# Attention over a graph's edges: tables in rows of 30 and 60, edges in two loads, a shorter last round with a branch behind it

## The chip, the cores and the metric

The kernel runs on one core of a Trainium2 chip. Its time is the device time of one execution in microseconds (us). TensorE (PE) multiplies matrices, VectorE (DVE) and ScalarE (ACT) work element by element, GpSimd (POOL) here mostly issues gathers, and SyncE (SP) issues the plain transfers. The core has 16 DMA engines; a transfer is split over some of them.

## The reference

One layer of graph attention over N = 12500 nodes with 256 features and E = 200000 edges, which come sorted by their target dst.

```python
h = jnp.maximum(_layernorm(x, axis=-1), 0.0)
q = (h @ Wq + bq).reshape(n, HEADS, D)          # HEADS 8, D 32
k = (h @ Wk + bk).reshape(n, HEADS, D)
v = (h @ Wv + bv).reshape(n, HEADS, D)
logits = jnp.einsum('ehd,ehd->eh', q[dst], k[src]) / jnp.sqrt(jnp.float32(D))
seg_max = jax.ops.segment_max(logits, dst, num_segments=n)
expv = jnp.exp(logits - seg_max[dst])
denom = jax.ops.segment_sum(expv, dst, num_segments=n)
attn = expv / denom[dst]
agg = jax.ops.segment_sum(attn[:, :, None] * v[src], dst, num_segments=n)
y = h + jax.nn.gelu(agg.reshape(n, HID) + (h @ Wskip + bskip), approximate=False)
return x + _layernorm(y) * gamma + beta
```

The sources src are drawn evenly over the nodes; dst is 12500 u² for u drawn evenly from 0 to 1, so the first nodes have many edges and the last ones few.

## The kernel before

**Three stages.** First, project (in gnn_kernel) makes h and, with 98 blocks of 128 nodes, the keys and values: two products of 128 x 512 a block on PE (L243), added to the bias by DVE into kvo, and stored as kv_tab and h_tab. Beside it make_plan works out from src and dst, mostly on DVE and POOL, who handles which edge when: load_edges reads the 200000 edges into 127 partitions of 1566 and a rest of 1118, DVE casts them (L418), indirect loads fetch for each step its first edges (dch from dst, sch from src), and from these come the lists of the gathers idx, the first node of each step and stream (d0_row), the rows of finished nodes (slot_row) and a flag, which SyncE and the others read at the end of the plan (values_load): it chooses between walk_streams and a general path, walk_partitions.

Second, walk_streams. The list of edges is cut into S = 8 streams of 25000, and the loop goes over c = 0 to 65 (NST = 66 steps); a step takes 383 new edges of every stream, as K = 3 tiles j of 128 (the last step has two). For each tile POOL issues eight indirect gathers, one for each stream, of 128 rows of keys and values (gather, L1010), into one of five buffers kv. Since dst is sorted, a step of one stream meets few target nodes: a window of 32 nodes in streams 0 to 3 ("narrow") and 64 in streams 4 to 7 ("wide"). windows loads their rows of h (hw), PE makes the queries from them, spread repeats these for the edges with one-hot matrices (to_e), times multiplies with the keys (DVE, L1053), total sums within heads (L1062), maxima finds the running maximum of a node's edges by two scans (L1082 is the first) and ACT takes the exponential, weigh multiplies the values by these weights into vw (L1109; L1114 is a small second product of the first tile), and add_up sums over the edges of a node with the other one-hot matrix (to_n) on PE. The sums are copied to sums_w and stored to table in DRAM: from each window all rows but the first, so 31 and 63 of them. A node cut by the boundary of two steps is carried on by copying row 0's sums into the next step.

```python
              keep(nc.sync.dma_start(table[s, ds(g["nodes"][s], w - 1), :],
                                     g["sums"][at + 1:at + w, i, :]))
```

A store writes rows of nodes beyond the step's last one as well; the next step overwrites them, so SyncE's stores to one part of table stay in order. The plan checks that no step meets more nodes than a store holds (far and bad in make_plan, against w - 1); otherwise the flag chooses the general path.

**Pairs.** A finished node still needs division by its sum, the skip product, gelu, the second normalization and the output store. These go by slots: 104 slots of 128 nodes, taken two at a time as 52 Pairs. Pair m is due in step FIN_FIRST + m * FIN_RATE // 32, that is from step 10 on in most steps one; its work is spread over three steps (fetch; turn, divisors, skip, divide, add, gelu, stats, root as "pair"; factors, normal, shifted, scale, store as "before"). The streams begin their blocks of 128 nodes anew, so the number of slots filled depends on where the streams' boundaries fall; it is counted in the plan (gvu[:, 0, F - 1:]), and slots beyond it repeat the last one. Pairs 46 to 51 come due only after the last step; the class Last handles these six, whose rows of x and h are loaded in step 64 (fetch_rows) and whose sums after the last stores (fetch_sums, L913).

**Order.** keep ties every instruction of the loop to the one before on its engine, so each engine works in the order in which the code is written. The gathers on POOL are outside keep, but POOL runs them in program order, and a gather waits until its buffer is free: the third of step c + 1, gather(c + 1, 2), stands behind weigh(c, 0). In the plan the order on each engine is instead made by a scheduler, which works from its own estimates of how long each instruction and transfer takes; some instructions of project are tied by hand (behind).

**The last round** (after the loop, c = 65): pair is m = 45 and before is m = 44. The order on every engine is: before.factors and normal; the one-hot products; before.shifted, scale, store(0); the last pairs' first turn; maxima; then exp, weigh and add_up, the stores of table; before.store(1); the fetches of sums; pair's ending; and the six last pairs, first all up to gelu, then all endings, two output stores for each (L882). The six take their PSUM banks from qe_ps (four), xt_ps and ag_ps (bank).

Of the kernel before, what the change touches and what calls it, by code (L numbers as in the profile page):

```python
# [28 lines left out]
F32 = mybir.dt.float32  # L29
# [22 lines left out]

FIN_FIRST = 10
FIN_RATE = 39
PAD = 127.0
# [8 lines left out]
def gnn_kernel(ctx: ExitStack, tc: tile.TileContext, x, src, dst, Wq, bq, Wk, bk, Wv, bv,  # L64
# [248 lines left out]
    flag = pl.tile([1, 2], I32, name="flag")  # L313
# [12 lines left out]
    fits = nc.values_load(flag[0:1, 0:1], min_val=0, max_val=1)  # L326
    with tc.If(fits > 0) as branch:
        table = dram.tile([S, NT, SUMS], F32, name="table")
        walk_streams(tc, N, HID, NST, KL, ident, idx, d0_row, slot_row, near, near_n, e_tab, pen_tab,
                     h_tab, kv_tab, table, x, out, w_q, w_s, one_row, b_q3, b_s3, b_o3,  # L330
                     gam, eps)
# [45 lines left out]
def load_edges(nc, pool, a, E, C, fill, name):  # L377
# [4 lines left out]
    nc.gpsimd.dma_start(t[:full], a[:full * C].rearrange("(p c) -> p c", c=C))  # L382
# [15 lines left out]
def make_plan(tc, pool, ep, psum, src, dst, N, LEN, NST, SLACK, NT, dram, ident, flag, idx, d0_row,  # L398
              slot_row, e_tab, pen_tab, products):

# [104 lines left out]
    for i, w in enumerate((WNN, WN)):  # L505
        nc.vector.tensor_scalar(bad[:, 0, i * 4:i * 4 + 4], bad[:, 0, i * 4:i * 4 + 4],
                                float(w - 1), None, op0=OP.is_gt)
# [108 lines left out]
    for i, w in enumerate((WNN, WN)):  # L616
        nc.vector.tensor_reduce(far[:, i:i + 1], dl[:, i * 4:i * 4 + 4, :], AX.XY, OP.max)
        nc.vector.tensor_scalar(far[:, i:i + 1], far[:, i:i + 1], float(w - 1), None,
# [51 lines left out]
    nc.vector.tensor_scalar(w2[:, 4:5], gvu[:, 0, F - 1:], float(M), None, op0=OP.is_gt)  # L670
    nc.vector.tensor_reduce(w2[:, 5:6], w2[:, 0:5], AX.X, OP.max)
# [69 lines left out]
def walk_streams(tc, N, HID, NST, KL, ident, idx, d0_row, slot_row, near, near_n, e_tab, pen_tab, h_tab,  # L741
# [174 lines left out]
    with ExitStack() as es:  # L916
# [199 lines left out]
        def add_up(c, i, tiles=range(K)):  # L1116
# [28 lines left out]
            for s in streams:  # L1145
                _, at, w = where(s)
                keep(nc.sync.dma_start(table[s, ds(g["nodes"][s], w - 1), :],
                                       g["sums"][at + 1:at + w, i, :]))
# [5 lines left out]
        rest = due.get(NST - 1, []) + due.get(NST, [])  # L1154

# [27 lines left out]
        assert len(rest) <= 6  # L1183
# [8 lines left out]
        def bank(i):  # L1192
            def get():
                if i > 3:
                    return (xt_ps.tile([P, 512], F32, name="ps_x") if i == 4 else
                            ag_ps.tile([P, 2 * HID], F32, name="ps_a")).rearrange(
                                "p (b d) -> p b d", b=2)
# [13 lines left out]
        for c in range(NST - 1):  # L1211
# [48 lines left out]
            if c == NST - 2:  # L1260
                for i in range(6):
# [51 lines left out]
        if before:  # L1313
            before.factors()
            before.normal()
# [6 lines left out]
        if before:  # L1322
            before.shifted()
        if tiles_of(c) == K:
            turn(c, K - 1)
        if before:
            before.scale()
            before.store(0)
        if pair:
            pair.divisors()  # L1330
# [414 lines left out]
```

## Time and profile before

| what | us |
|---|---|
| median of 15 runs (lowest, highest) | 2402.76 (2393.57, 2417.73) |
| the profiled execution, its own time | 2398.33 |
| its span in the profile | 2396.5 |
| busy: PE, DVE, POOL, ACT | 1866.0, 1935.0, 1593.1, 1076.7 |
| 1576 gathers on POOL (L1010) | 1548.7 |
| 197 large products of weigh on DVE (L1109) | 444.7, 2.285 each |
| 394 products of times on DVE (L1053) | 467.8, 1.219 each |

The span is the time from the first to the last instruction in the profile; the execution's own time is a little longer. A group's row in the profile gives its busy time, the mean of one instruction, and the idle time of its engine just before, with what ended most of it. A wait is put down to the last of the events that the instruction needed. The chain of waits is followed back from the end: at each step to what released the instruction, or to the one before it on its engine. POOL issues the gathers, and between two of them lies issue time that is not counted as busy. A transfer's row gives its issue; when it has landed is read from what waits for it, or from the semaphore that its engines count up.

### The profile page before, as it was taken

To read this page: it belongs to the slowest core of one execution; us is meant where nothing else is said; L and a number is where in the kernel's file an instruction comes from. 1 tells how busy PE (TensorE), PEld (TensorE's weight loads), DVE (VectorE), ACT (ScalarE), POOL (GpSimd) and SP (SyncE) were. 2 spreads that over 40 slices of the span, in tenths; PEclk is the share of its full clock that TensorE was granted. 3 is DMA by queue.
4 is the path that set the end of the run, shared out by engine and by line. 5 is a ranking of instruction groups with operands and counts; after the bars stand their busy time and mean duration, and the time that the engine had idled before them with its cause. 6 is when DMAs were issued, how large, how long until landed. Compare 5 with 4: busy or idle time off the path is not lost.

```text
span 2396.5 us, 34967 instructions
## 1 busy us (share of the span) xinstructions
PE 1866.0 (78%) x10240; PEld 1077.8 (45%) x10240; DVE 1935.0 (81%) x2228; ACT 1076.7 (45%) x2527; POOL 1593.1 (66%) x1646
## 2 busy tenths in 40 slices
PE   7999776777877787777777787877787777787776
PEld 3444443444444444444444444444444444444443
DVE  7889577777788878778788888788788888788784
ACT  3432233333455445445455454454454554454443
POOL 2210677777777777777777777777777777777730
PEclk9999778777899889889999898898988998988987
DMA  7865777778877878887888888887888888788862
GB/s 276 301 248 206 239 244 244 243 244 256 261 251 252 266 251 257 271 259 245 262 263 255 270 261 260 263 269 240 267 258 266 259 267 256 255 269 256 260 194 69
DMA packets 274030, 601.06 MB, mean 251 GB/s; under 512 B 47239, under 2 KB 164212, under 8 KB 271648
## 3 DMA queue, kind: packets, MB, share of 16 engines
q0 software_dynamic: 128736, 423.23, 55.9%
q1 hardware_dynamic: 144562, 175.02, 21.9%
q8 instruction: 84, 1.38, 0.2%
q14 instruction: 118, 0.97, 0.1%
q10 hardware_dynamic: 530, 0.47, 0.1%
HBM read 514.42 MB, written 84.11 MB: 250 GB/s over the span
## 4 chain that ended last, share of the span: by engine, by line
POOL 25%; DMA 23%; DVE 18%; PE 15%; issue 14%; ACT 4%; DVEq 0%; SPq 0%; ACTq 0%; POOLq 0%
POOL kv L1010 25%; DMA kv<-kv_tab,idx 20%; DVE vw L1109 6%; PE ps_kv L243 5%; DVE prod L1053 5%; PE ps_qe L1043 3%; DVE L L1062 2%; PE ps_a L829 2%; PE ps_hot L871 1%; DVE st L845 1%; DMA x_in<-in_x_dram 1%; ACT L950 1%; DMA e_tab<-row 1%; DMA table<-sums_w 1%; DVE sums L841 1%
## 5 line engine op out<-in xcount | busy, mean ns | idle before, releaser
L1010 POOL DMA_INDIRECT kv<-kv_tab,idx x1576 | 1548.7, 983 | 522.6 <-issue 428.1
L1043 PE MATMUL ps_qe<-qw,to_e 64*128 64x256 f32 x3152 | 484.3, 438 | 227.0 <-DVE prod L1053 227.0
L1109 DVE TENSOR_TENSOR vw<-ps_x,kv 128x2048 f32<-128x2048 f32 x197 | 444.7, 2285 | 162.9 <-ACT vw L1102 162.9
L1053 DVE TENSOR_TENSOR prod<-ps_qe,kv 128x1024 f32<-128x1024 f32 x394 | 467.8, 1219 | 118.6 <-DMA kv<-kv_tab,idx 99.4
L1043 PEld LDWEIGHTS ps_qe<-qw,to_e 64*128 64x128 f32 x3152 | 307.2, 207 | 385.1 <-DVE prod L1053 346.0
L1062 DVE TENSOR_REDUCE L<-prod 128x64 f32<-128x2048 f32 x197 | 450.3, 2286 | 6.7
L1003 PE MATMUL ps_hot<-w_q,hwT 128*128 128x256 f32 x792 | 244.4, 452 | 1.0 <-ACT hwT L989 0.8
L1128 PE MATMUL ps_a<-vw,to_n 128*32 128x264 f32 (+1 forms) x2344 | 218.5, 401 | 3.9 <-DVE vw L1114 2.9
L1033 ACT ACTIVATE to_n<-ps_hot,ones 128x384 f32<-128x384 f32 x197 | 107.1, 578 | 218.7 <-PE ps_hot L1031 218.6
L243 PE MATMUL ps_kv<-w_kv,hT 128*128 128x512 f32 x392 | 186.8, 620 | 21.7 <-ACT hT L136 20.7
L1003 PEld LDWEIGHTS ps_hot<-w_q,hwT 128*128 128x128 f32 x792 | 161.5, 219 | 87.3 <-issue 59.8
L1137 ACT COPY sums_w<-ps_a 128x264 f32<-128x264 f32 x130 | 49.2, 378 | 333.2 <-PE ps_a L1128 333.2
L950 ACT ACT_TABLE_LOAD x138 | 177.1, 1283 | 2.4
L1005 ACT COPY qw<-ps_hot 128x256 f32<-128x256 f32 (+1 forms) x132 | 63.2, 479 | 235.4 <-PE ps_hot L1003 234.1
L1022 ACT ACTIVATE to_e<-ps_hot,ones 128x384 f32<-128x384 f32 x264 | 143.7, 587 | 6.3 <-PE ps_hot L1020 6.1
L1143 ACT COPY kv<-ps_a 1x264 f32<-1x264 f32 x388 | 143.0, 369 | 6.3
L1128 PEld LDWEIGHTS ps_a<-vw,to_n 128*32 128x32 f32 (+1 forms) x2344 | 87.6, 119 | 125.4 <-issue 73.6
L989 ACT COPY hwT<-ps_hot 128x256 f32<-128x256 f32 (+1 forms) x132 | 63.5, 481 | 161.2 <-PE ps_hot L986 158.7
L1020 PE MATMUL ps_hot<-et,near 48*128 48x384 bf16 x264 | 89.9, 341 | 41.3 <-ACT qw L1005 25.6
L829 PE MATMUL ps_a<-w_s,hT 128*128 128x256 f32 x368 | 110.5, 452 | 14.6 <-ACT hT L815 13.2
L243 PEld LDWEIGHTS ps_kv<-w_kv,hT 128*128 128x128 f32 x392 | 72.1, 194 | 105.7 <-issue 71.3
L1093 PE MATMUL ps_x<-ident,W 64*128 64x64 f32 x197 | 29.7, 266 | 100.4 <-ACT W L1086 100.4
(292 smaller groups left out, 2180.2 us busy)
## 6 DMA issues: line engine op xcount, KB each, us to landing
kv<-kv_tab,idx POOLq DMA_INDIRECT x1576
kv_tab<-kvo SPq DMA_DIRECT2D x14, 1536.0 KB
table<-sums_w SPq DMA_DIRECT2D x264, 65.0 KB
hw<-h_tab SPq DMA_DIRECT2D x264, 64.0 KB
pen<-pen_tab SPq DMA_DIRECT2D x66, 192.5 KB
sums<-table SPq DMA_DIRECT2D x92, 132.0 KB
x_f<-in_x_dram SPq DMA_DIRECT2D x92, 128.0 KB
h<-h_tab SPq DMA_DIRECT2D x92, 128.0 KB
```

What stands on the lines that cost most here:

```text
L243: ins = nc.tensor.matmul(ps_kv, hT[:, c, :], w_kv[:, c, :], start=c == 0, stop=c == KC - 1)
L829: self.keep(nc.tensor.matmul(self.ps[:, b, :], self.hT[:, b, c, :], w_s[:, c, :], start=False, stop=False, skip_group_check=True))
L950: keep(nc.scalar.activation(dummy[:, 1:2], dummy[:, 0:1], function))
L1003: keep(nc.tensor.matmul(ps[:, b, :], g["hwT"][:, b, k, :], w_q[:, k, :], start=False, stop=k == KC - 1, skip_group_check=True))
L1010: nc.gpsimd.indirect_dma_start(out=t[:, s, :], out_offset=None, in_=kv_tab[:, :], in_offset=bass.IndirectOffsetOnAxis(ap=idx[:, s, j, c:c ...
L1022: keep(nc.scalar.activation(step[c]["to_e"][:, i, :], ps[:, :CH], AF.Relu, scale=-1.0, bias=ones))
L1043: keep(nc.tensor.matmul(ps[:, b, a, :], g["to_e"][r, 2 * half + a, j * P:(j + 1) * P], g["qw"][r, (half + a) * half, :], start=True, stop= ...
L1053: keep(nc.vector.tensor_tensor(g["prod"][:, four, :].rearrange("p (a b) d -> p a b d", a=2), g["qe", half].rearrange("p b a d -> p a b d") ...
L1062: keep(nc.vector.tensor_reduce(g["L"][:, j, :].rearrange("p (s h) -> p s h", s=S), g["prod"].rearrange("p s (h d) -> p s h d", h=HEADS), A ...
L1109: keep(nc.vector.tensor_tensor(t[:, :, HEADS:].rearrange("p s (h d) -> p s h d", h=HEADS), wj[:, :, :, None].to_broadcast([P, S, HEADS, D] ...
L1128: keep(nc.tensor.matmul(ps[at:at + w, :], g["to_n"][:, j, i * P + at:i * P + at + w], g["vw"][j][:, s, :], start=j == 0, stop=j == tiles_o ...
L1143: keep(nc.scalar.copy(step[c + 1]["kv"][0][0:1, s, HID - HEADS:], ps[at:at + 1, :]))
```

## The change

It has four parts.

1. **Rows of a store.** A store of sums takes 30 rows in the narrow streams and 60 in the wide ones (USED) in place of 31 and 63. The plan's two checks use the same numbers, so a step with more nodes than that sets the flag for the general path. The windows themselves stay 32 and 64 wide.
2. **Loads of the edges.** load_edges reads its 127 full rows in two transfers, 112 rows and 15, for each of src and dst.
3. **The last round.** maxima stands right after the one-hot products; before's steps are spread behind it: factors after pair.divide, normal and shifted after weigh(0), scale after the last add_up, its stores and pair's together ahead of the last pairs' divisions. The last pairs' turn and skip move too, and there are four of them (46 to 49), all with banks of qe_ps.
4. **Two pairs behind a branch.** Pairs 50 and 51 (from SURE = 50 on) run only if the plan counted more than 100 slots: a third word of flag (many), loaded into a register like the first, decides by tc.If at the very end. They run as plain Pairs, one step after another.

```diff
--- before.py
+++ after.py
@@ -50,8 +50,12 @@
 NARROW = {0: 0, 2: 32, 1: 64, 3: 96}
 WNN = 32
 
+USED = {WNN: 30, WN: 60}
+
 FIN_FIRST = 10
 FIN_RATE = 39
+
+SURE = 50
 PAD = 127.0
 
 ROOM = 128
@@ -310,7 +314,7 @@
     NSLOT = (NBLK + S - 1) // 2 * 2
     assert NSLOT <= P
     pl = ctx.enter_context(tc.tile_pool(name="plan", bufs=1))
-    flag = pl.tile([1, 2], I32, name="flag")
+    flag = pl.tile([1, 3], I32, name="flag")
     idx = pl.tile([P, S, K, NST], I32, name="idx")
     d0_row = pl.tile([1, NST * S], I32, name="d0_row")
     slot_row = pl.tile([1, NSLOT // 2, 4], I32, name="slot_row")
@@ -324,9 +328,10 @@
         make_plan(tc, pool, ep, psum, src, dst, N, LEN, NST, SLACK, NT, dram, ident, flag,
                   idx, d0_row, slot_row, e_tab, pen_tab, products)
     fits = nc.values_load(flag[0:1, 0:1], min_val=0, max_val=1)
+    many = nc.values_load(flag[0:1, 2:3], min_val=0, max_val=1)
     with tc.If(fits > 0) as branch:
         table = dram.tile([S, NT, SUMS], F32, name="table")
-        walk_streams(tc, N, HID, NST, KL, ident, idx, d0_row, slot_row, near, near_n, e_tab, pen_tab,
+        walk_streams(tc, N, HID, NST, KL, many, ident, idx, d0_row, slot_row, near, near_n, e_tab, pen_tab,
                      h_tab, kv_tab, table, x, out, w_q, w_s, one_row, b_q3, b_s3, b_o3,
                      gam, eps)
     with branch.Else():
@@ -379,7 +384,10 @@
     t = pool.tile([P, C], I32, name=name)
     full, rest = divmod(E, C)
     nc.vector.memset(t, fill)
-    nc.gpsimd.dma_start(t[:full], a[:full * C].rearrange("(p c) -> p c", c=C))
+
+    for lo, hi in ((0, full // 16 * 16), (full // 16 * 16, full)):
+        if lo < hi:
+            nc.gpsimd.dma_start(t[lo:hi], a[lo * C:hi * C].rearrange("(p c) -> p c", c=C))
     if rest:
         nc.gpsimd.dma_start(t[full:full + 1, :rest], a[full * C:].rearrange("(p c) -> p c", p=1))
     return t
@@ -504,7 +513,7 @@
     nc.vector.tensor_sub(bad[:, 0], nn[:, 1:], line[:, 1, :])
     for i, w in enumerate((WNN, WN)):
         nc.vector.tensor_scalar(bad[:, 0, i * 4:i * 4 + 4], bad[:, 0, i * 4:i * 4 + 4],
-                                float(w - 1), None, op0=OP.is_gt)
+                                float(USED[w]), None, op0=OP.is_gt)
     cnt = pool.tile([1, 1, S], F32, name="cnt")
     nc.vector.tensor_sub(cnt[:, 0], nn[:, 1:], nn[:, :S])
     nc.vector.tensor_scalar(bad[:, 1], cnt[:, 0], float(P), None, op0=OP.is_lt)
@@ -615,7 +624,7 @@
     far = pool.tile([NST, 2], F32, name="far")
     for i, w in enumerate((WNN, WN)):
         nc.vector.tensor_reduce(far[:, i:i + 1], dl[:, i * 4:i * 4 + 4, :], AX.XY, OP.max)
-        nc.vector.tensor_scalar(far[:, i:i + 1], far[:, i:i + 1], float(w - 1), None,
+        nc.vector.tensor_scalar(far[:, i:i + 1], far[:, i:i + 1], float(USED[w]), None,
                                 op0=OP.is_ge)
     nc.vector.tensor_max(worst[:NST, 1:2], far[:, 0:1], far[:, 1:2])
     nc.vector.tensor_scalar(real, real, -PAD, PAD, op0=OP.mult, op1=OP.add)
@@ -668,6 +677,7 @@
     nc.vector.tensor_reduce(w2[:, 2:3], bad, AX.XY, OP.max)
     nc.vector.tensor_reduce(w2[:, 3:4], late[:, 1], AX.X, OP.max)
     nc.vector.tensor_scalar(w2[:, 4:5], gvu[:, 0, F - 1:], float(M), None, op0=OP.is_gt)
+    nc.vector.tensor_scalar(flag[:, 2:3], gvu[:, 0, F - 1:], float(2 * SURE), None, op0=OP.is_gt)
     nc.vector.tensor_reduce(w2[:, 5:6], w2[:, 0:5], AX.X, OP.max)
     nc.vector.tensor_scalar(flag[:, 0:1], w2[:, 5:6], -1.0, 1.0, op0=OP.mult, op1=OP.add)
 
@@ -738,7 +748,7 @@
                                             op0=OP.mult)
 
 
-def walk_streams(tc, N, HID, NST, KL, ident, idx, d0_row, slot_row, near, near_n, e_tab, pen_tab, h_tab,
+def walk_streams(tc, N, HID, NST, KL, many, ident, idx, d0_row, slot_row, near, near_n, e_tab, pen_tab, h_tab,
                  kv_tab, table, x, out, w_q, w_s, one_row, b_q3, b_s3, b_o3, gam, eps):
 
 
@@ -1144,14 +1154,16 @@
                                         ps[at:at + 1, :]))
             for s in streams:
                 _, at, w = where(s)
-                keep(nc.sync.dma_start(table[s, ds(g["nodes"][s], w - 1), :],
-                                       g["sums"][at + 1:at + w, i, :]))
+                keep(nc.sync.dma_start(table[s, ds(g["nodes"][s], USED[w]), :],
+                                       g["sums"][at + 1:at + 1 + USED[w], i, :]))
 
         due = {}
         for m in range(NPAIR):
             due.setdefault(min(NST, FIN_FIRST + m * FIN_RATE // 32), []).append(m)
         assert all(len(ms) == 1 for c, ms in due.items() if c < NST)
         rest = due.get(NST - 1, []) + due.get(NST, [])
+        extra = [m for m in rest if m >= SURE]
+        rest = [m for m in rest if m < SURE]
 
         prefetch(0)
         windows(0)
@@ -1180,7 +1192,7 @@
                 spread(0, j + 1, half)
             total(0, j)
             turn(0, j)
-        assert len(rest) <= 6
+        assert len(rest) <= 4
         lasts, banks = [], {}
 
         def room(i):
@@ -1191,10 +1203,6 @@
 
         def bank(i):
             def get():
-                if i > 3:
-                    return (xt_ps.tile([P, 512], F32, name="ps_x") if i == 4 else
-                            ag_ps.tile([P, 2 * HID], F32, name="ps_a")).rearrange(
-                                "p (b d) -> p b d", b=2)
                 if i % 2 == 0:
                     banks[i // 2] = qe_ps.tile([P, 2, 2, HID], F32, name="ps_qe")
                 return banks[i // 2][:, i % 2]
@@ -1258,7 +1266,7 @@
             if before:
                 before.store(1)
             if c == NST - 2:
-                for i in range(6):
+                for i in range(4):
                     last(i)
             if pair:
                 pair.add()
@@ -1310,39 +1318,31 @@
                 step[c - 2] = None
 
         c = NST - 1
-        if before:
-            before.factors()
-            before.normal()
         for j in range(tiles_of(c)):
             if tiles_of(c) == K and j < 2:
                 times(c, K - 1, j)
             hot_n(c, j)
             if tiles_of(c) == K and j == 1:
                 total(c, K - 1)
-        if before:
-            before.shifted()
         if tiles_of(c) == K:
             turn(c, K - 1)
-        if before:
-            before.scale()
-            before.store(0)
-        if pair:
-            pair.divisors()
-        for p in lasts[:1]:
-            p.turn()
         maxima(c)
         if pair:
             table_of(AF.Gelu)
+            pair.divisors()
             pair.divide()
+        if before:
+            before.factors()
         turn_back(c)
         weights(c)
         weigh(c, 0)
         if pair:
             pair.add()
             pair.gelu()
+        if before:
+            before.normal()
+            before.shifted()
         for p in lasts[:1]:
-            p.skip()
-        for p in lasts[1:2]:
             p.turn()
         for j in range(1, tiles_of(c) - 1):
             weigh(c, j)
@@ -1353,15 +1353,12 @@
             p.find_sums()
         for i in range(3):
             add_up(c, i, range(tiles_of(c) - 1, tiles_of(c)))
+        for p in lasts[:1]:
+            p.skip()
         if before:
-            before.store(1)
+            before.scale()
         for p in lasts:
             p.fetch_sums()
-        for p in lasts[1:2]:
-            p.skip()
-        for p in lasts[2:4]:
-            p.turn()
-            p.skip()
         if pair:
             pair.stats()
             pair.root()
@@ -1370,21 +1367,18 @@
             pair.shifted()
             pair.scale()
             table_of(AF.Gelu)
-        for p in lasts[4:5]:
+        for p in lasts[1:]:
             p.turn()
             p.skip()
-        if pair:
-            pair.store(0)
-            pair.store(1)
-        for i, p in enumerate(lasts):
+        for p in (before, pair):
+            if p:
+                p.store(0)
+                p.store(1)
+        for p in lasts:
             p.divisors()
             p.divide()
             p.add()
             p.gelu()
-            if i == 1:
-                for p in lasts[5:]:
-                    p.turn()
-                    p.skip()
         table_of(AF.Sqrt)
         for i in range(len(lasts) + 2):
             if i < len(lasts):
@@ -1398,6 +1392,17 @@
                 lasts[i - 2].scale()
                 lasts[i - 2].store(0)
                 lasts[i - 2].store(1)
+        if extra:
+            with tc.If(many > 0):
+                for m in extra:
+                    p = Pair(fin, m, lambda: hot_ps.tile([P, 2, KC, P], F32, name="ps_hot"),
+                             lambda: ag_ps.tile([P, 2 * HID], F32, name="ps_a").rearrange(
+                                 "p (b d) -> p b d", b=2), lambda ins: ins)
+                    for stage in (p.fetch, p.turn, p.skip, p.divisors, p.divide, p.add, p.gelu,
+                                  p.stats, p.root, p.factors, p.normal, p.shifted, p.scale):
+                        stage()
+                    for b in range(2):
+                        p.store(b)
 
 
 def walk_partitions(tc, src, dst, N, NP, HID, ident, flag, q_tab, kv_tab, table, dram):
```

## The prediction

> **What bounds the kernel now.** I read the page first, then busy time by three stretches, then the waits of the middle stretch, then the chain, the timeline and SyncE's own waits at the end.
>
> ```profile
> span 2396.5 us, 34967 instructions
> L1010 POOL DMA_INDIRECT kv<-kv_tab,idx x1576 | 1548.7, 983 | 522.6 <-issue 428.1
> 0.00:245.50 245.50, 211.29 (x619) 99.85 (x620) 204.87 (x551) 86.93 (x217) 44.33 (x70) 0.99 0.70 257
> 245.50:2307.00 2061.50, 1596.32 (x9370) 942.52 (x9368) 1679.21 (x1571) 957.44 (x2243) 1548.74 (x1576) 0.88 0.81 257
> 2307.00:2396.50 89.50, 58.40 (x253) 35.47 (x253) 50.88 (x107) 32.30 (x67) 0.00 (x0) 0.77 0.31 98
> ```
>
> Columns of the last three: length, then busy time of PE, weight loads, DVE, ACT, POOL, then clock and DMA. The first stretch is projection and plan (PE 211 of 245), the second the loop, the third the end. In the loop POOL issues 24 gathers a step, a typical one 0.95 us and 0.30 us of issue: 24 x 1.255 = 30.1 us. The gather starts show just that for steps 0 to 10 (30.16 to 30.20), and about 31.3 on average from step 12 on, where pairs are finished. So POOL sets the pace, and a step is longer for two reasons: POOL's own records lengthen (47 us over the loop, beside DVE work that touches no store), and POOL waits.
>
> ```profile
> DVE prod L1053 <- DMA kv<-kv_tab,idx: 99.4, 43, 6.1
> POOL kv L1010 <- DVE vw L1114: 38.3, 21, 3.8
> SPq L977 <- DMA table<-sums_w: 198.3, 207, 3.6
> SPq L882 <- DMA out_dram<-kv: 15.3, 11, 2.6
> 1840.60 8.94 DMA table<-sums_w
> ```
>
> (Waits in us, times, longest; the last line is a piece of the chain.) POOL's waits are 32.6 us once the issue time is taken off: the buffer for gather(c+1, 2) is free only after weigh(c, 0), L1114. That work hangs on times(c, 2), and DVE sits idle there for the landing of the step's last gather. The landing is late because of the 31-row stores: the trace's semaphore counts show that each is landed by one DMA engine, each 63-row store by nine. In 51 of the 64 steps, fifteen engines have finished the step's last gather about 3.3 us after POOL's record of it ended and the sixteenth at 5 to 6.8; in the steps where the stores were issued later than that gather (or within about 0.2 us before its end) all sixteen are done at about 2.4.
>
> The end:
>
> ```profile
> 2329.29 0.63 DVE L1082 TENSOR_TENSOR_SCAN ps_x<-pen,ps_x 64x256 f32<-64x256 f32 x1
> 2339.97 3.60 SPq L1147 DMA_DIRECT2D table<-sums_w  x8
> 2349.47 8.68 SPq L913 DMA_DIRECT2D kv<-table  x12
> 2370.32 21.80 SPq L882 DMA_DIRECT2D out_dram<-kv  x12
> 2382.71 0.69 DVE L877 TENSOR_TENSOR kv<-kv,ps_hot 128x512 f32<-128x512 f32 x1 [0.41 <-PE ps_hot L871]
> ```
>
> DVE is done at 2383.4, but twelve output stores go out one after another, each waiting until the one before has landed: from 2370.32 to 2392.1, 1.95 us apart on average, mostly 1.75.
>
> **Part 1, stores of 30 and 60 rows.** Eight stores a step as before, no instruction more; what changes is how many engines carry one. The trace before has no 30-row store. Bounds: the old one (the four of the last round landed 3.4 to 6.7 us after their issue) and a 128-row output store (about 1.7 us, 2372.13 to 2373.83). Nearest in rows is the 32-row load hw<-h_tab, counted on sixteen engines, landing in about 3; I take 2.7. [...] So the last gather lands at about 3.3 instead of 6.2. What this is worth is bounded step by step: POOL gains no more than its own wait, and no more than DVE's idle time for that gather in the same step. The sum of the smaller of the two over all steps is 25.6 us (waits 32.6, DVE idle there 103). **-25**, bounds 0 (another wait takes over) and -32.6. SyncE's 198 us for these stores free nobody: waits put down to the loads hw<-h_tab add up to 3.1 us between 320 and 2276. Steps 0 to 10 gain nothing, since POOL never waits there though DVE does.
>
> **Part 2, edges as 112 and 15 rows.** One more POOL issue for each of two tables, 0.55 us (row L384), in POOL's idle time: it waits 16.25 us before the second load and 15.67 before dch. The 127 rows are spread already (127 packets of 0.40 us land within 5.9 us), so the load gains nothing. What can move is the planner's order. DVE's cast of the edges, L418, stands at 69.48, though they landed at 13.3: it was placed for a late load. Placed earlier, the whole plan moves forward. But PE ends this stretch: 98 blocks at 2.22 us are 217.6 from 10.0, that is 227.6, against 241.7, so 14.1 are lost, of which some 8.6 in the ramp up to 40 us, and 4.4 at 115, where DVE waits 4.30 us for sch<-src_p and evacuations queue behind it. An early plan can remove the latter (-5, and 0.7 at the first gather, which starts 0.9 us after the last landing it needs), or put waits for edges at DVE's head during the ramp, with kvo and the statistics behind them (+9: load from 3.28 to 13.3). I take **+1**, since the ramp is already short of input.
>
> **Part 3, the last round.** Maxima at once: in the old order L1082 stood behind before.factors, normal, shifted and scale and began at 2329.29; its input, the last transpose, is done at 2321.5. Exp then follows both to_n copies on ACT (in turn from 2324.05): 2325.2 instead of 2331.1, -5.9. weigh(0) from 27.4 instead of 33.3 (2300 left out from here). add_up is held back once: the third PSUM tile waits for before.scale, now behind weigh(1), 32.05 + 1.4; add_up is done at 35.7 instead of 40.5. Stores from 35.2, eight at 0.45, the last landed at 41.0; the old fetch of sums began at 49.47 after SyncE had waited for the one-engine stores. But PE is the longer way: skip 2.4, shifted 1.5, three times turn and skip 3.1 (2343.2 to 2346.3), some waiting for ACT's table loads: the first add at 49.7 instead of 53.9. Four pairs take 6.3 us to the last gelu (56.0), six took 11.0 (64.96). From there to the first store 5.34 as before (64.98 to 70.32): 61.3. Eight stores at about 1.77: the last is issued at 73.7 instead of 92.1. **-18**. The four stores of before and pair go out from 46.7 to 52.4, ahead of that. Bounds: -10 (the clock in this stretch is 0.77, and 8 products take 2.0 or 3.8 us) and -22. SyncE also issues 8 loads fewer from 2306 on (0.6 each); nobody waits there.
>
> **Part 4, the branch.** many is one more register load on each engine at 240 (0.5 to 0.8), on SyncE behind the load of flag at 240.93, ahead of the last kv_tab store at 242.64: hidden; uncovered it costs 0.8. One tensor_scalar on DVE, 0.14. From the reference's inputs the eight streams hold 195, 584, 989, 1367, 1751, 2153, 2521 and 2940 nodes; in blocks of 128 that is 2+5+8+11+14+17+20+23 = 100, not over 100, so the two pairs are skipped, and the windows need at most 26 and 53 rows, so the streams' path is kept. Skipping is a taken branch at the end of each engine. The outer one, on SyncE, lasts from 2392.18 to 2394.9, 2.7 us; a compare that stays in line took 0.05. **+1.5**, bounds 0 and 4. [...]
>
> **The sum**: -25 + 1 - 18 + 1.5 = -40.5. The profiled execution took 2398.3 (span 2396.5), 4.4 below the median of the runs shown, 2402.8. So 2357.8 for one like it, and 2362 beside the median.
>
> **Rivals.**
> 1. The loop stays as it is: DVE starts earlier, but ACT and PE hold weigh(c, 0) back, as in the steps where PE runs at half speed (in the longest steps DVE idles 4.6 us before L1109). For it: DVE's wait for vw there is 161 us in all, more than for gathers. Against: DVE's idle time stands before that in the same chain. 2362 + 25 = 2387.
> 2. The loop gains all its waits and the early plan its 5.7: -32.6 - 18 + 1.5 - 5.7 = -54.8: 2348.
> 3. Slower: the planner, now thinking the edges early, places the plan's casts where their data isn't there yet. DVE works in order, so each such wait stops kvo, and PE after its four banks. Price: edges 10 us twice, dch and sch 25 (99.33 to 124), gvu 10, d0 7: some 62 if all are exposed, 7 of which are now. It decides from 48 exposed, where 2362 becomes 2410. Against: 84 us of plan on DVE cost only 5 so far.
> 4. It doesn't do what it says: the two pairs run after all. Each alone, from these rows: loads 6, skip 4, add and gelu 3, statistics and root 3.6, the rest 3, stores 4, about 23, so some 46: 2408.
>
> **Chances.** Forecast 0.64 (2351 to 2374), first rival 0.17, second 0.11, third 0.05, fourth 0.03. About 0.3%, 7 us, can be told from no change. Faster: forecast, first and second, less 0.03 for a first rival with the short end: 0.89. Within: fourth, half of that and some of the third, 0.06; slower 0.05. The range is 2343 (all low bounds but the end's) to 2390 (first rival with 3 us at the branch).
>
> **What would show it.** A landing of all sixteen parts of the step's last gather within about 3.5 us; POOL's wait for L1114 under 15 us and gather steps of 31.2; L1082 of the last round 8 us after the last product there; eight stores at the end, first issued some 9 us earlier counted from the last gather; the projection ending near 242. It is wrong if the steps stay at 31.3 on average, if the projection ends past 250, or if a long stretch follows the last store.

## The result: 61 us faster, just below the forecast range

| | us |
|---|---|
| before, median of 46 runs (lowest, highest) | 2402.47 (2393.57, 2417.73) |
| changed, median of 9 runs (lowest, highest) | 2341.81 (2338.28, 2348.53) |
| ratio | 0.9746, 95% interval 0.9727 to 0.9764 |
| profiled executions: before, changed | 2398.3, 2348.2 |

By the medians the change takes off 60.7 us where 40.5 were forecast, and 2341.8 lies 1.2 us below the range (2343 to 2390). The profile of the changed kernel: its page (two lines) and the busy time in the same three stretches (length, then PE, weight loads, DVE, ACT, POOL, granted clock, DMA).

```profile
span 2346.4 us, 34800 instructions
L1020 POOL DMA_INDIRECT kv<-kv_tab,idx x1576 | 1541.2, 978 | 493.8 <-issue 438.7
0.00:246.05 246.05, 211.23 (x619) 99.78 (x620) 205.10 (x552) 86.98 (x217) 45.11 (x72) 0.99 0.71 256
246.05:2270.61 2024.56, 1585.20 (x9378) 936.02 (x9376) 1681.12 (x1572) 957.63 (x2243) 1541.20 (x1576) 0.88 0.83 261
2270.61:2346.44 75.83, 45.70 (x201) 26.71 (x201) 40.38 (x82) 27.35 (x57) 0.00 (x0) 0.75 0.25 81
```

The first stretch has its old length (+0.5), the loop lost 36.9 us (2061.5 to 2024.6) and the end 13.7 (89.5 to 75.8): 50.1 between the two profiled executions. The other 10.6 us are in which execution of each kernel was profiled: before's lies 4.1 us below its median, the changed one's 6.4 above.

The waits of the changed kernel in its loop (us, times, longest), DVE's and POOL's, and SyncE's longest:

```profile
DVE prod L1063 <- DMA kv<-kv_tab,idx: 82.5, 41, 5.2
DVE o L887 <- PE ps_hot L881: 40.0, 44, 2.8
POOL kv L1020 <- DVE vw L1124: 4.4, 4, 2.5
SPq L1157 <- ACT kv L1153: 820.5, 128, 30.5
```

POOL's wait for the small product of weigh (L1114, now L1124) is nearly gone: over its issue time POOL waited 32.6 us before and 3.3 now. SyncE's 198 us of waits for stores of table (L977) are gone from its list; its longest wait is for the sums themselves, as it was before (598 us, L1147), only longer. DVE still waits 82.5 us for gathers: it has caught up with POOL, and waits at POOL's pace. By the semaphore counts, each store of 30 or 60 rows is now landed by fifteen engines, where one of 31 rows was landed by one and one of 63 by nine. The sixteenth engine ended a step's last gather 5.9 us (median of the steps) after POOL's record before, and 3.8 now, the fifteenth at 3.3 and 3.6. The steps' gathers start 30.97 us apart from step 12 on, where they started 31.67 apart (the prediction's 31.3 "on average" is near the median, 31.2).

The end of the changed kernel (start, length, engine, line):

```profile
2283.01 0.70 DVE L1092 TENSOR_TENSOR_SCAN ps_x<-pen,ps_x 64x256 f32<-64x256 f32 x1 [1.24 <-PE ps_x L1081]
2303.37 5.60 SPq L923 DMA_DIRECT2D kv<-table  x8
2323.74 16.53 SPq L892 DMA_DIRECT2D out_dram<-kv  x8
2329.64 0.69 DVE L887 TENSOR_TENSOR kv<-kv,ps_hot 128x512 f32<-128x512 f32 x1 [0.41 <-PE ps_hot L881]
```

Counted from the last gather's end (2306.96 before, 2270.61 now): the scan of maxima starts at 12.4 instead of 22.3, the fetch of the sums at 32.8 instead of 42.5, the first output store at 53.1 instead of 63.4, the last is issued at 69.3 instead of 84.8.

### The profile page after: what moved, and what is told of

Its sections match the earlier page's. It is cut to its first block, busy times and chain, and to the rows that moved or that the text cites. A ratio compares the mean times of both kernels' runs of the same rounds, so it can differ in the third digit from the quotient of the medians.

```text
span 2346.4 us, 34800 instructions
## 1 busy us (share of the span) xinstructions
PE 1842.1 (79%) x10196; PEld 1062.5 (45%) x10196; DVE 1926.6 (82%) x2205; ACT 1072.0 (46%) x2517; POOL 1586.3 (68%) x1648
## 4 chain that ended last, share of the span: by engine, by line
POOL 31%; DMA 18%; issue 16%; DVE 16%; PE 14%; ACT 3%; SPq 1%; DVEq 0%; POOLq 0%; ACTq 0%
POOL kv L1020 31%; DMA kv<-kv_tab,idx 14%; DVE vw L1119 5%; PE ps_kv L247 5%; DVE prod L1063 5%; PE ps_qe L1053 4%; DMA e_tab<-row 2%; DVE L L1072 1%; PE ps_a L839 1%; PE ps_a L1138 1%; DMA x_in<-in_x_dram 1%; PE ps_hot L1013 1%; PE ps_hot L881 1%; DVE ps_x L1092 1%; DVE st L855 1%
## 5 line engine op out<-in xcount | busy, mean ns | idle before, releaser
L1053 PE MATMUL ps_qe<-qw,to_e 64*128 64x256 f32 x3152 | 468.5, 426 | 199.9 <-DVE prod L1063 199.4
L1063 DVE TENSOR_TENSOR prod<-ps_qe,kv 128x1024 f32<-128x1024 f32 x394 | 467.4, 1219 | 98.5 <-DMA kv<-kv_tab,idx 82.5
L1053 PEld LDWEIGHTS ps_qe<-qw,to_e 64*128 64x128 f32 x3152 | 297.1, 200 | 354.3 <-DVE prod L1063 315.4
L1013 PE MATMUL ps_hot<-w_q,hwT 128*128 128x256 f32 x792 | 257.0, 471 | 1.0 <-ACT hwT L999 0.8
L1013 PEld LDWEIGHTS ps_hot<-w_q,hwT 128*128 128x128 f32 x792 | 169.5, 229 | 90.5 <-issue 60.5
L1147 ACT COPY sums_w<-ps_a 128x264 f32<-128x264 f32 x130 | 49.2, 378 | 326.8 <-PE ps_a L1138 326.8
```

The lines of the kernel that those rows point to most:

```text
L1013: keep(nc.tensor.matmul(ps[:, b, :], g["hwT"][:, b, k, :], w_q[:, k, :], start=False, stop=k == KC - 1, skip_group_check=True))
L1053: keep(nc.tensor.matmul(ps[:, b, a, :], g["to_e"][r, 2 * half + a, j * P:(j + 1) * P], g["qw"][r, (half + a) * half, :], start=True, stop= ...
L1063: keep(nc.vector.tensor_tensor(g["prod"][:, four, :].rearrange("p (a b) d -> p a b d", a=2), g["qe", half].rearrange("p b a d -> p a b d") ...
```

## The experiments

Theory at the start: the whole gain of the loop comes from the stores of 30 rows, which no longer land by one engine; the end gives 14 us and the edges nothing. The rival: the rows give the forecast 25 us and the other parts the rest.

**Each part alone.** The rows: the kernel before with

```diff
-                keep(nc.sync.dma_start(table[s, ds(g["nodes"][s], w - 1), :],
-                                       g["sums"][at + 1:at + w, i, :]))
+                keep(nc.sync.dma_start(table[s, ds(g["nodes"][s], USED[w]), :],
+                                       g["sums"][at + 1:at + 1 + USED[w], i, :]))
```

and USED in the plan's two checks. The edges: the kernel before with the loop over 112 and 15 rows in load_edges. The end: the changed kernel with

```diff
-USED = {WNN: 30, WN: 60}
+USED = {WNN: 31, WN: 63}
```

and the one load of 127 rows. Without the branch: the changed kernel with

```diff
-    NSLOT = (NBLK + S - 1) // 2 * 2
+    NSLOT = 2 * SURE
```

so that more than 100 slots set the flag for the general path.

> The kernel before with part 1 alone: stores of 30 and 60 rows. Theory (the whole gain of the loop is that the last gather of a step no longer lands behind one-engine stores): POOL's waits over its issue time fall from 33 us to under 6, the gather steps average 31.0, and the median is some 45 us below the kernel before (60.7 less 14 at the end and 1 elsewhere), about 2357. Rival (the loop gains the 25 us that were forecast, and what came on top belongs to the other parts): the median falls by 25 to 30, about 2375, and steps average 31.3.

> The kernel before with part 2 alone: edges in 112 and 15 rows. Theory: the same as before within 3 us; the first gather starts near 246 and the projection ends near 242. Rival (the plan moves forward and the loop starts earlier, or gains from another order): 6 us or more below before. Its profile is also a second look at the old loop: POOL's waits over the issue time should be near 33 us and the stretched records near 47, if the profiled execution of before was typical.

> The changed kernel with stores of 31 and 63 rows and the edges in one load of 127 rows: parts 3 and 4 alone. Theory: the last stretch, from the last gather to the end, takes some 76 us instead of 89.6, and the median is 14 us below before, about 2388; the loop is the old one, with POOL's waits near 33 us. Rival (fewer loads in step 64 and another end give the loop something too): 20 us or more below before.

> The changed kernel with 100 slots in all, so without the two spare pairs and their branch (more than 100 slots set the flag for the general path instead). Theory: what lies between the issue of the last output store and the end shrinks by some 1.8 us, from 6.2 to 4.4, and nothing else changes: the median lies 0 to 4 us below that of the changed kernel, 2338 to 2342, which can hardly be told. Rival (the branch costs more than the profile shows, through a register held on every engine or code loading): 6 us or more below.

These four ran on a chip on which the kernel before took 3738 us (median of 35). Against it the rows gave a ratio of 1.002 (0.9999 to 1.0041), the edges 1.000 (0.998 to 1.002), the end 0.9947 (0.9928 to 0.9967), the version without the branch 0.9965 (0.9939 to 0.999). What was different there, from the page and PE's waits of the kernel with the rows alone:

```profile
span 3738.9 us, 34967 instructions
PEclk9986666667767776777766777776767776677667
L1012 POOL DMA_INDIRECT kv<-kv_tab,idx x1576 | 1527.5, 969 | 1855.0 <-DVE vw L1116 1358.1
PE ps_a L1130 <- issue: 459.2, 275, 6.9
PE ps_qe L1045 <- issue: 367.4, 275, 5.6
```

The granted clock is 0.6 to 0.7 where the first profiles have 0.8 to 0.9, PE idles 827 us ahead of two groups of products without a wait that the profile shows, and POOL waits 1358 us for DVE. PE sets the pace there, a step takes 52 us, and a landing 2 us earlier is worth nothing. So these ratios do not tell the theories apart. (The granted clock alone does not make such a time: the light kernels below have 0.68 and take some 2400 us.) But two things can be read in their profiles. The edges alone start the first gather at 251.94, the other three at 252.83 to 253.07, so no more than some 1 us. The edges alone were not run at the full pace, that is on a chip on which the kernel before takes some 2400 us. And without the branch the kernel ends 4.6 us after the issue of its last output store, where the changed kernel takes 6.5 and the kernel before 4.8: the branch costs 1.8 us.

Two more kernels have USED as 29 and 60, and as 30 and 59. Both have fewer rows than the change, but 29 and 59 are primes like 31, whose stores were landed by one engine.

> Stores of 30 and 60 rows alone, on another chip than before if one is given. Theory (the gain of the loop is that the last gather of a step no longer lands behind one-engine stores): where POOL sets the pace, POOL's waits over its issue time fall from 33 us to under 6, and the median is some 45 us below before, about 2357. Rival (25 us as forecast, the rest from the other parts): 2375.

> Parts 3 and 4 alone (31 and 63 rows, one load of 127). Theory: from the last gather to the end some 76 us instead of 89.6, the loop as before with waits of POOL near 33 us; median 14 us below before, about 2388. Rival (the new order also eases the loop): 20 us or more below.

> The changed kernel with 29 rows in the narrow stores in place of 30: one row less, but a prime number, the wide ones stay at 60. Theory (what counts is how many engines carry a store): the four narrow stores are each landed by one engine again, the last gather of a step by its sixteenth engine at 5 to 6.8 us, POOL waits some 30 us, and the time is that of parts 3 and 4 alone, about 2385. Rival (fewer rows and bytes, or the wide stores alone): within 5 us of the changed kernel, 2342.

> The changed kernel with 59 rows in the wide stores in place of 60: a prime number, narrow ones stay at 30. Theory: each wide store is landed by one engine and takes about twice as long as a 31-row store did, 7 to 13 us; the last gather of a step lands later than in the kernel before, POOL waits over 33 us, and the time is above that of parts 3 and 4 alone: 2390 to 2440, so the gain of the change is gone with fewer rows than it has. Rival (fewer rows and bytes do it): within 5 us of the changed kernel.

> Stores of 30 and 60 rows alone, a third time, for a chip whose TensorE is granted the clock of the first profiles (0.89, not 0.72). Theory there: POOL's waits over its issue time under 6 us in place of 33, median some 45 us below before. Rival: 25 to 30 us below. If the granted clock is 0.72 again, PE sets the pace and both theories expect no difference (within 0.3%).

The same low clock, on two other chips: before 3744 and, for the last, 3764 us; rows 1.0007 (0.999 to 1.0024) and 1.0002 (0.9976 to 1.0028), the end 0.9938 (0.9914 to 0.9963), 29 rows 0.9945, 59 rows 0.9966. They repeat what the first four said and leave 29 and 59 undecided; 59 was not run elsewhere.

**A lighter PE**, to have POOL set the pace even at a low clock: to_e, qw, to_n and vw in bf16, with 31 and 63, with 30 and 60, and with 29 and 60 rows.

```diff
-            g["qw"] = hold.tile([P, 3, HID], F32, name="qw")
+            g["qw"] = hold.tile([P, 3, HID], BF16, name="qw")
```

> The kernel before with the operands of two products of the loop (spread and add_up) in bf16 instead of f32: to_e, qw, to_n and vw. It computes the same with less precision and needs far less of PE. Expected: PE's busy time falls from 2320 us to under 1700 and its clock rises above the 0.72 of the last runs, so that POOL sets the pace again: gather steps of 30 to 32.5 us instead of 52, about 2400 us in all. If PE still set the pace, steps would stay over 35 us.

> The same with stores of 30 and 60 rows. Theory (one-engine stores hold back the step's last gather): POOL's waits over its issue time fall to under 6 us, from the 10 to 35 us of the kernel with 31 and 63 rows, and the time falls by these waits and up to 10 us more from the stretched records: 15 to 45 us less than it. Rival (with a quicker PE the landing is hidden): within 7 us of it.

> The same with 29 rows in the narrow stores, a prime number, and 60 in the wide ones. Theory (what counts is the number of engines that carry a store): each narrow store is landed by one engine, and most of the gain of 30 rows is gone: within 10 us of the kernel with 31 and 63 rows. Rival (fewer rows, or the wide stores, do it): within 5 us of the kernel with 30 and 60.

On this chip the kernel before took 2399.9 us again. The light kernels took 2409.2, 2392.4 and 2414.8 us: 30 rows give 16.8 us, and with 29 the gain is gone. The sixteenth engine ended a step's last gather at 5.7, 3.3 and 5.6 us. The expected waits fell short: over its issue time POOL waited 48.8, 40.0 and 53.5 us. And the clock did not rise with less work on PE: it was granted at 0.68. In the light kernels 180 of the 184 products of shifted (L881 of the changed kernel) take over 0.6 us (0.63 at the median, where the quickest take 0.38); in the kernel before 72 do, in the changed one 36. With the light rows, DVE waits only 3.8 us for gathers between 620 and 2280, so DVE's own chain is likely what holds POOL there, and an early landing has less to give.

**The parts on a chip at the full pace.** The chip on which it had taken 3764 us ran the kernel before in 2402.2 us 18 minutes later.

> Stores of 30 and 60 rows alone, on a chip on which the kernel before takes 2400 us. Theory (the gain of the loop is that the step's last gather no longer lands behind one-engine stores): POOL's waits over its issue time under 6 us in place of 33, median some 45 us below before. Rival (25 us as forecast, the rest from the other parts): 25 to 30 us below.

> Parts 3 and 4 alone, on such a chip. Theory: from the last gather to the end some 76 us instead of 89.6, the loop as before, POOL's waits near 33 us; median 14 us below before. Rival (the new order eases the loop as well): 20 us or more below.

> The changed kernel with 29 rows in the narrow stores, on such a chip. Theory (the number of engines that carry a store counts): the sixteenth engine lands the step's last gather at 5 to 6.8 us again, POOL waits some 30 us, and the time is that of parts 3 and 4 alone, some 14 us below before. Rival (fewer rows and bytes): as the changed kernel, some 60 us below before.

| kernel | median, us | less than before | ratio (interval) | loop | last gather to end | POOL's waits over issue | lengthened records | 16th engine |
|---|---|---|---|---|---|---|---|---|
| before | 2402.2 | | | 2061.4 | 89.6 | 32.6 | 47.3 | 5.9 |
| rows alone | 2361.8 | 40.4 | 0.9844 (0.9815 to 0.9873) | 2021.3 | 87.8 | 0.7 | 39.0 | 3.8 |
| end alone | 2388.3 | 13.9 | 0.9939 (0.9921 to 0.9957) | 2063.3 | 79.2 | 37.6 | 44.7 | 6.05 |
| changed, 29 rows | 2379.1 | 23.1 | 0.9908 (0.9873 to 0.9942) | 2056.2 | 79.1 | 33.1 | 42.1 | 6.0 |
| changed (first runs) | 2341.8 | 60.7 | 0.9746 (0.9727 to 0.9764) | 2024.6 | 75.8 | 3.3 | 39.8 | 3.8 |

(Loop, end and the last columns are of one profiled execution each, for the kernel before the one shown at the start; "lengthened" is what POOL's gather records take over 0.953 us, and the last column is the median landing of the step's last gather.) POOL's waits and DVE's wait for the xb of shifted, in the rows alone, the end alone and the 29 rows:

```profile
POOL kv L1012 <- issue: 440.2, 1444, 0.3
POOL kv L1012 <- DMA kv<-kv_tab,idx: 22.6, 74, 0.3
DVE o L879 <- PE ps_hot L873: 40.1, 45, 2.8
```

```profile
POOL kv L1018 <- issue: 432.5, 1419, 0.3
POOL kv L1018 <- DVE vw L1122: 42.9, 20, 4.8
DVE o L885 <- PE ps_hot L879: 58.1, 44, 2.8
```

```profile
POOL kv L1020 <- issue: 438.4, 1433, 1.9
POOL kv L1020 <- DVE vw L1124: 36.3, 16, 4.9
DVE o L887 <- PE ps_hot L881: 54.1, 44, 2.8
```

With 30 rows there is no line of a wait for vw among POOL's largest; with 29, which moves less, there is the old one. By the semaphore counts each 29-row store is landed by one engine again, and the 60-row ones beside them by fifteen. Number of engines, not size, decides: that part of the theory is shown, for the narrow stores. (That the late sixteenth engine is the one that lands the stores is not told by the counts; that one is late only where stores land on one engine, the eight profiles of 2346 to 2409 us show.) The rows alone give 40.4 us, less than the theory's 45 and just outside what 25 to 30 would allow (interval 30 to 44, from four runs); the end alone 13.9, and its loop is the old one. The two add to 54.3, the change gave 60.7; their intervals (the end's is 10 to 19) leave that open. With 29 rows the kernel keeps some 9 us over the end alone, with intervals that overlap (14 to 31 us and 10 to 19); whether the wide stores on fifteen engines are worth something by themselves was not told apart.

**Why fewer records are lengthened.** The four lines that follow are of step 20 of the kernel before: POOL's seventeenth gather of the step waits for the small product of weigh, and its last one starts just after add (L841) and takes 1.47 us.

```profile
883.26 2.29 DVE L1109 TENSOR_TENSOR vw<-ps_x,kv 128x2048 f32<-128x2048 f32 x1 [4.58 <-ACT vw L1102]
885.83 0.95 POOL L1010 DMA_INDIRECT kv<-kv_tab,idx  x1 [3.80 <-DVE vw L1114]
894.58 0.68 DVE L841 TENSOR_TENSOR sums<-sums,h 128x512 f32<-128x512 f32 x1
894.63 1.47 POOL L1010 DMA_INDIRECT kv<-kv_tab,idx  x1 [0.31 <-issue]
```

This happens in 18 steps of that kernel, and in all 18 POOL had waited for its buffer: the wait sets POOL's gathers in step with DVE, and the seventh gather after it starts 0.03 to 0.05 us after add. It costs 0.5 us each time, 9.2 us in all; with the change 2.8 us (6 gathers) are left, with the rows alone 0.9 (2), with the end alone 9.3 (18), with 29 rows 8.2 (17). So most of the fall in lengthened records is a second price of the same waits.

**What the lengthened records are worth.** 40 us of them are left. Here is one, of the changed kernel:

```profile
1766.34 1.80 POOL L1020 DMA_INDIRECT kv<-kv_tab,idx  x1 [0.30 <-issue]
1766.64 0.67 DVE L828 TENSOR_TENSOR o<-sums,den 128x512 f32<-128x512 f32 x1
```

A gather beside divide (L828) takes 1.80 us instead of 0.95. Two kernels were to say whether that sets the pace of the steps with a pair: one with a further subtraction on DVE ahead of divide, one with the chain from maxima to weigh made shorter.

```diff
-                pair.divisors()
...
             if pair:
-                table_of(AF.Gelu)
+                pair.divisors()
                 pair.divide()
             turn_back(c)
             weights(c)
+            if pair:
+                table_of(AF.Gelu)
```

> The changed kernel once more, on the chip of the two that follow and with a second profile. Expected 61 us below before, by the medians; and if the first profiled execution of it was only a slow one of its kind (it took 2348, the median 2342), the second shows gather steps a little shorter than 30.97 us and the same stretches elsewhere.

> The changed kernel with one more subtraction on DVE (64x384, like L1095, result unused) ahead of pair.divide in the loop, where DVE waits 2 us for ACT afterwards. In the traces a gather is stretched by up to 0.85 us when divide starts in its first 0.4 us, and not at all when it starts at 0.4 to 0.7; this moves divide by some 0.5. Theory A (what is left of the loop over 30.2 us a step is these stretches): stretched time falls from 40 us to under 20 and the time by 15 to 35 us. Theory B (in the steps with a pair DVE's own chain of 31.2 us sets the pace, and the stretches only use up POOL's lead): stretched time falls, POOL waits that much longer for its buffer, and the time stays within 5 us.

> The changed kernel with ACT's table load for gelu behind the copies of weights instead of ahead of them, and divisors behind maxima, in the loop: on the chain from maxima to weigh this takes out some 1.0 us of ACT and 0.45 us of DVE in each step with a pair. Theory B (that chain sets the pace in these steps): steps of 31.2 us become 30.2 to 30.6, and the time falls by 15 to 35 us. Theory A (stretched gathers set it): within 7 us of the changed kernel.

These ran at the low clock again (before 3762 us), on the very chip that had run before in 2402. The changed kernel gave 0.9985 (0.9971 to 0.9999), the shifted divide 0.9976 (0.9962 to 0.999), the short chain 0.9724 (0.9701 to 0.9748): 3660 us against 3756. For the question asked this decides nothing, since POOL does not set the pace there, and neither the second profile of the changed kernel nor the worth of the records was got. But it shows what holds the steps at the low clock: DVE's wait for ACT ahead of weigh falls from 155.0 to 83.0 us, and the loop by 94.

```profile
DVE vw L1119 <- ACT vw L1112: 83.0, 66, 3.1
POOL kv L1020 <- DVE vw L1124: 1301.4, 63, 34.9
```

(Waits of the short chain.) So at the low clock this version beats the changed kernel by 2.6% and the kernel before by 2.8%; at the full pace it was not run.

## Why the prediction was right in kind and too small

**The loop, where it failed.** The forecast named the mechanism, and its signs came: POOL's waits, steps under 31.2, and the sixteenth engine, if at 3.8 us and not within 3.5. That stores of 30 and 60 rows would be carried by more engines was an estimate, shown by no run at the time; the changed kernel's counts show fifteen for both. The term was mis-sized: 25 us, at most 32.6. The rows alone took 40.1 off the loop's profile, 31.9 in POOL's waits (32.6 to 0.7) and 8.3 in records that are lengthened less (47.3 to 39.0). In the changed kernel it was 36.9: 29.3 in waits and 7.5 in records. So two steps of the prediction failed, the smaller one by 4.3 to 6.9 us and the larger by 7.5 to 8.3.

The first is "the sum of the smaller of the two over all steps", with DVE's idle time for the gather in the same step as a ceiling; POOL's own wait, the other ceiling, held. In step 20 of the kernel before POOL waited 3.5 us while DVE had waited only 1.5 for the gather: DVE then waited 2.8 for shifted's product and 4.6 for ACT, where other steps have 0.57 and 2.04. Of these later waits the one for shifted's product shrank with the early landing; the one for ACT did not, summed over the loop (161 us before, 165 with the change). In the kernels with a late landing 64 to 72 of the 184 products of shifted take over 0.6 us, with an early one 31 and 36; DVE's wait for them is 54 to 60 us with the one and 40 with the other. Before it was

```profile
DVE o L877 <- PE ps_hot L871: 60.4, 44, 2.8
```

That these go together is shown by five profiles. In the two of them that are of the kernel before and the changed one, the granted clock is 0.50 during each of these products that takes over 0.6 us (0.63 to 0.80; 72 before, 36 with the change) and 1.00 during all the others (0.38 to 0.48). That it is PE's idle time, while DVE waits, that brings the lower clock was the author's inference and is not shown; the light kernels' lower clock at less work (0.68 with PE busy for 1619 us, against 0.89 and 1866) agrees with it in direction. The first rival spoke of just these steps, but took the half speed for something that stands beside the landing; much of it went with it.

The second is the lengthened records: they were seen beforehand (47 us), and the sum put their change at nothing without a reason. They fell by 7.5 in the changed kernel and by 8.3 with the rows alone, and 2.6 with the end alone, and most of that fall, 6.4 and 8.3 us, is beside add, in steps in which POOL had waited.

**Edges and plan.** +1 forecast, +0.5 seen. The planner left the cast nearly where it was: it starts at 69.99, before at 69.48. The projection ends at 241.72, before at 241.71. The third rival, casts placed too early, did not come, nor the second one's early plan.

**The end.** -18 and +1.5 for the branch forecast; 13.8 in all came in the profile, 10.4 with the end alone, 13.9 by its median. Up to the first output store the steps hold: 53.1 after the last gather, forecast 54.3. Then eight stores were costed at 1.77 us each; they were issued 2.3 us apart on average, three of them only 2.9 to 3.2 us after the one before, and the last stood at 69.3 instead of 66.7. The branch cost 1.8, forecast 1.5, an estimate between the 0.05 and 2.7 us that compares took in the kernel before: SyncE runs nine semaphore instructions of the skipped If, 1.75 us from its branch to the outer one, and the outer branch still takes its 2.7.

**The offset.** The forecast set the sum against the profiled execution and added 4.4 for the median, as if the next profile would lie as far below its own. It lay 6.4 above: 10.8 us of the 20 that were missed. The range had nothing for that, though before's runs shown reached from 2394 to 2418. Nor does its lower edge come out of its own description: all low bounds but the end's give 2346.5, and 2342.5 with the end's. The rest of the miss is the loop (+11.9) less the end (-2.7) and the plan.

**The others.** The loop did not stay (first rival), the two pairs did not run (fourth). Nearest was the second, 2348: nearly all waits gone; but 5.7 of its 54.8 us are an early plan that did not come, so its nearness is in part luck.

## What to carry to other kernels

Look at how many engines land a transfer before looking at its bytes: 30 and 60 rows (fifteen engines each) in place of 31 and 63 (one and nine) took 40 us off 2402, and with 29 (one engine) in place of 30 most of the gain was gone. The waits of the engine that sets the pace (32.6 us) bounded what their removal gave (29.3 and 31.9); the idle time for the landing, in the same step, did not, since a wait downstream of it, for shifted's product, shrank as well. A wait can also set two engines in step (in 18 steps here, 9.2 us), so look at what is lengthened in the steps with a wait. And a forecast against a median needs the spread between executions in its range, since the profiled one can lie on either side.

## What the runs showed of the hardware

- Within 27 minutes the same chip ran the same kernel in 3764, in 2402 and again in 3762 us, with a granted clock near 0.72, 0.88 and 0.72; at 0.72 single products of add_up stood idle for 0.8 to 2.2 us (one step of the rows alone) with nothing to wait for that the profile shows, and the change that gave 2.5% gave 0.15%. What brings this about was not found.
- With two products in bf16 and less work on PE (busy for 1619 us, against 1866) the granted clock was lower (0.68, against 0.88 of the kernel before on that chip) and the kernel 0.4% slower: 180 of the 184 products of shifted, which stayed in f32, took over 0.6 us, where 72 had.
- A POOL gather beside divide on DVE took up to 1.91 us instead of 0.95; in the five profiles of the table it depended on when within the gather divide began (0.56 to 0.96 us longer when in its first 0.41 us, none from 0.44 on).
